# First attention of a two-layer block, from tokens on partitions to channels on partitions

## The chip, the cores and the metric

The kernel runs on one core of a Trainium2 chip. The core has five engines with a queue each: TensorE (PE; its weight loads are listed apart as PEld), VectorE (DVE), ScalarE (ACT), GpSimd (POOL) and SyncE (SP), which here only issues transfers. An engine works its queue off in order and waits on semaphores where an instruction needs another engine's result. Sixteen DMA engines move data between DRAM and the on-chip memory SBUF; TensorE writes to the banks of PSUM.

The metric is the device time of one execution in microseconds, as the median over runs. Before the change it is 2111.85 us (18 runs, 2101.27 to 2121.52).

## What is computed

Two layers with a layer norm after each sublayer, over 16 sequences of 512 tokens and 128 channels, in float32:

```python
x = L0_attn_x
x = _layernorm(x + _L0_attn_ref(x, ...), axis=-1)
x = _layernorm(x + _L0_ffn_ref(x, ...), axis=-1)
x = _layernorm(x + _L1_attn_ref(x, ...), axis=-1)
x = _layernorm(x + _L1_ffn_ref(x, ...), axis=-1)
```

The change is in the first attention. It has 16 heads of 64 value channels, 1024 in all, and is linear in time:

```python
cross = jnp.einsum('bnw,hw->bhn', x, k1) + p1
diag = jnp.einsum('bnw,hw->bhn', x, k2)
extra = jnp.einsum('bnw,hw->bhn', x, k3)
values = jnp.einsum('bnw,hwa->bhna', x, value_weight)
cexp = lambda z: jnp.exp(jnp.clip(z, -20.0, 20.0))[..., None]
cross, diag, extra = (cexp(cross), cexp(diag), cexp(extra))
p2e = cexp(p2)
num = jnp.cumsum(cross * values, axis=2) * p2e * extra + values * diag
den = jnp.cumsum(cross, axis=2) * p2e * extra + diag
out = num / den
return jnp.einsum('bhna,hwa->bnw', out, output_weight)
```

The running sum goes over the tokens of a sequence (axis 2). Every gate (`cross`, `diag`, `extra`, `p2e`, and so `1/den`) is one number for each head and token, the same for the head's 64 channels. The other sublayers are a mixture of eight experts with one expert a token, a softmax attention of 16 heads with a position bias, and a second mixture with a shared expert. They are not changed.

## The kernel before

The kernel does not run the sublayers one after the other. Every piece of work is an `op` with an engine, a planned cost and the tiles that it reads and writes, and all are issued in one order, which is written out as a long string, `ORDER` (L54 to L206): two characters for each op give its rank. Each engine gets its ops in that order. The string comes from a search outside the kernel; nothing of it is computed at build time. When an op is added or removed, the whole string is another one.

The sequences go in chunks (`CHUNKS`, L32: 2, 3, 4, 3, 3 and 1). `first` runs the first attention and first mixture of a chunk, `second` its softmax attention and what the shared expert needs, `mixture1` the routed part of the second mixture. The first layer of chunk c+1 is woven into the second attention of chunk c, so that both share the engines: only chunk 0's first layer has nothing beside it but the setup, and after the last chunk's first layer the second attention runs on without it.

Tiles come from pools with a fixed number of buffers (L285 to L311). The ones that matter here: `pair`, two banks of PSUM, 3 buffers; `wide`, 128x1024 float32 in SBUF, 12 buffers; `one`, one bank of PSUM, 2 buffers; `row`, 128x512 in SBUF, 11 buffers. They are shared by all sublayers.

The first attention of a sequence is `attention0`, then four tiles of 128 tokens by `tile0`. Tokens lie on the partitions. `attention0` makes the gates as 128 tokens x 4 tiles x 16 heads: scores (L952 to L957), exponentials in `ex`, prefix sums of `cross` by products with a triangle of ones (`ce`, L966 and L968), and from these `gg` = p2e·extra/den and `own` = diag/(cross·den) (L976 to L990). `tile0` then does for each tile of 128 tokens:

- `pv` (L1015, PE): values of all 1024 channels, two products 128x512
- `ev` (L1028, DVE): values times `cross`, the gate repeated over a head's 64 channels by a stride of 0
- `self_` (L1034, POOL): `ev` times `own`
- from the second tile on, the last row of the tile before (`carry`, L1057, ACT) is added into row 0 of `ev` by an accumulating transfer that POOL issues (L1041)
- `cum` (L1050, PE): running sum along the tokens, a product with the triangle `tri`
- `o` (L1062 and L1066, DVE): `cum` times `gg`, plus `self_`
- `po` (L1073, PE) and `ot` (L1076, ACT): eight transposes, so that channels lie on partitions, and a copy
- `y` (L1081, PE) and the residual add (L1089, DVE): eight products 128x128 with the output weights, added to `x`

So the tiles of one sequence form a chain: tile t+1 needs the carry of tile t.

The second attention, which shares the engines with it, works in rounds: 16 a sequence, four groups of heads times four tiles of keys. A round has its scores (`st`, L1422, PE), the bias added (`p`, L1441, DVE), the exponential (L1447, ACT) and the weighted sum (`av`, L1456, PE), beside a pass in low precision that finds the maxima (`s`, L1308 and L1317, PE; `low`, L1333, ACT, and L1349 to L1377, DVE). q and k of a group are moved into place by SP (L1272, L1285), and the maxima go the same way (`mx`, L1405): the scores of a group wait for that last transfer of 8 KB, which is planned 1.5 rounds ahead (`EARLY`, L41). GpSimd issues the indirect transfers of the mixtures (L796): expert weights, and rows of tokens there and back.

Of the kernel before, what the change touches and what calls it, by code (L numbers as in the profile page):

```python
# [19 lines left out]
P = 128  # L20
# [34 lines left out]
    "#$###)#9#-#0#.#&#%#(#A#D#'#,#B#G#J#=#7#H#I#K#*#?#L#M#O#F#P#Q#R#W#X#Y#6#C#T#U#Z#<#>#S#a#d#@#3#[#i"  # L55
    "#k#N#4#^#f#m#`#g#l#n#o#t#{#}#/#2#1$-#s#x$4$2$/$c#_#5#r&:#+#:#;%H'Y#u#8#v#w#V#]#b#~$#$$#c#p$'$&$+"
    "$)$*$0$3$:$A#e#z$,$.$7$9$8$<$B$E$K$]$1$6$;$?$D$H$L$M$N$[$a$e$C$G$I$J$T$U$W$Y$b$h$u$y%'%J%Q%R%W%["
    "%l#E#|$F$O$P$S$V$Z$Q$R$f$X$^$`$g$j$k$q%5$_$d$i$m$n$o$v$w$x${%*%@$l$p$r$s$|%,%)%+%-%2%E%M$z%$%(%."
    "%/%6%8%<%A%B%K%N%S%X%Y%^%`%b%c%d%e%f%m&8&Q&q'2&9&?&>&G&H&I&U&Y'.&E&o&R&Z&t&{&}&~'5'$'&'%'3'>'@'P"
    "'['e'#']'T'V'h'n't'u'v(/(2(4(=(@(d(r(s*>+T#y#h#j#q$%$($5$=$t%w$>%1&7%v'A'f(I(G%y'*&i%x$@$}%z'B(>"  # L60
    ")5'?-.(K%t(B(C(S(W(D(O(T(P(N(Y)>)&)d)=(U(x(q(V([)T)e)S)g)<)J)K({(~)$)Q)*)+)-(l(z(})E)1)6)9)C)G)I"
    ")X)m)3):)@)/)2)4)H)r)u*)*;*L)')F(e(k)?)f)c*P*Z*T*U*f*_*w*})O)V)^)Y)Z)j)v*|*`*c*{+'+-+9)W)])i)7)8"
    ")D)x*o*n*t++*u+/+A)N)P)U)(),)0*,*3*z+#+(+>*~+8+K*(***0*#*$*'*5*6*7*S*[+&+N+Q+Y)a)b)R)`+*+5+I+4+G"
    "+H+L+_+P+[+k*:*=*@)s)t)y*A+@+R+X+a+D+W+p*<*B*E)w)z)|*F+E+`+d+s+F+Z+}*C*D*I*4*8*9*J*K+6+g+l+x+;+C"
    ",*)p)~*&*+*/*1*p*q*r*x*y+J,0,4,<*.*-*G*%+h,/,&+n,,+b+f+o,1,8,9*M*Y*^*g*h*i+0+r+w+z,2+v+{,:*]*a*b"
    "*d*e*l+=+i+|,#,@+m+y,C*k*m*s+$+%+.+2+B,%,),5,E,',3,P+1+:+?+)+7+<+O+U+c+t,$,(,X,],`,W,A,F,S,Z,b,m"
    ",N,O,U,d,R,g,w,l,Q,T,[,n,p,~,^,_,i,v,a,j-+-1-5-=-E-[-_-t-u.).8.J.K.u.}.W.r.[.`.x/5/;1H,+,-,e,f,."
    ",7,=,>,D,B,;,M,?,r,H,K,V,L,J-8,s-9-W-/-4-<-2-3-;-O,u,{,}-'-)-0-K-?-A-C,|-#-*-Q-X-&-(-,,h,o,x-R-Y"
    "-Z.$.%.+,I,z,y,q-I---:-V.A.@.I.L.D.Y.c-L-P-`-6-@-B-m.M.S.U.a.O.X.p-d-f-h-J-M-]-p.Q.d.g.s.V.b.~-G"
    "-S-^-e-i-l-n-o.k.h.m.n.t.y/E-a-c-g-s-x-y-z.0.3.B.G.^/F/O/b-U-T-k-H/R.q/V/T/#/I/J/_/'/B/f.,.-.5-v"  # L70
    "-}-~/,/?/K/Q/^/G/H/p.>.E.H./.=.?.j/M/`/g/r/W/d/{.w.z.{.v.|/%/-/./o/h/k/s/v/}/~.e.f.i.6.7.9.l///0"
    "/@/D/j0#0005._.C-{.Z0$0%0+0,/y/w/x0;0)0K0O/$/&/)/*/+/1/<070*0/0J090I0U/(/2/6/[/a/e/i/z030?0Z0.0E"
    "0]/4/8/=/7/>/C/P/U0A0H0P0_0G0Q0b/L/N/]/X/c/q0'0(060=0F0L0q0u0z0W0M0S0T0X0`0k0N0R0V0a0^0h0l0[0i0r"
    "0t0m0o0|0d0n0y1%0v1'1(1)1,1.1415181@1A1C1N1Q1R1^1a1]1b1`1d1g2s3-:{$~%#%%%&%0%4%7%9%3%:%;%?%I%C%D"
    "%F%O%a%i%=%>%L%P%V%_%Z%]%o%{%|&.%T%U%g%h%j&$%n%u&&&'&)&+%p%q%s&%&*&/&2&3&6&=&S'8'F'Z(.(1(8(H%k%r"
    "%G%}%~&#&,&1&;&(&-&A&0&5&<&B&C&F&j&k&4&@&J&K&L&N&V&W&[&c&d&p&D&M&O&P&a&f&g&h&l&r'1'7&`&e&s&w&x&y"
    "&z'+'4':'G'H'L'i'}(#(g(m&X&T&]&^&_&b&u&v&m&n&|'''-'(')'6'9'M'N','/'='D'E'O'J'K'Q'S'a'k';'<'I'R'W"
    "'X'_'`'g'y'z($'U'^'p'q'w'x'|'~()(+(,(-(E(X(f(h(n(u(w(|)%).)[)k*?+~/:/A*R*j*v+,+M+V+e+j-7*Q+q+]+^"
    ",6,G,Y,k.*+3-%-D-F-q-w.;.</Y-b.P...:/3/9/S/Z/t/l/m/n/|0102080>0C0D0{0~1#1+0x1w1x424H1B2Q2m4^5R1j"
    "1y2.221k1l2F3#1m3$3=3;3W3[3]3_3c3d3g3m4%7)3X4*3z3{4?4B4@4L4M4X4e8:4{5D5k5l5s6u5y6/6w7h7q7s6`8(7v"  # L80
    "7y9a9s9i9j9t:2:F:[;s=I>/DhDiI@IA<;=9=T>5>??QBg/u10132b3'161=1:1<171D1G1c1r1s1F1v1L1|1J1u2'3J2~2C"
    "2G2K2L2P2W2p2=2@2B2D2E2J2d2M2V2Z2X2]2f3%322^2_2i2j2l2q3435363I3Q3R1[1P1O1T1~3b1q1}3k3e3j3t3n3v4&"
    "2,2/211o2#2$294)3p3u4+4.464:252:2;1f1h1i2<3l4345473o3x4C1z1{2(2024262R2S404;4A4I484F4T232>2?2H2I"
    "2N2O2T2U383G3P4Y4[4`2`2c2|2}4N4Q4G4R4V3w3y4>4Z4f4i3(3*3+2z3,313D4D4$4-4K4P4a4m2o2t2w373<3@3E4_4W"
    "4]4s4b4t5&303:3>3A3B3F3K3L4j4g4o4z4k4w5'2u2y3&3.3/393M3N3O4/4<4S5,54582Y2A2e2r4p4u4l4q4c5%5+514d"
    "4v592g2h2k2a2v2x334n5)5.524}5(5@3H3T3Y3S3U3a3f555*5-535:5;5A3h3i3q3V3Z3^3s3|4x505>5F4y5$5J3}3~4#"
    "4'4(4,444E4J4h4r4|5K5P5b5G5<5?5d5L5`5~5Q5E5N5V5S5u6$5}5x5{6'6#606;5T6%6.635e5t6R6Z6h6i7#7:7D7E7F"
    "7L7u7}7~9r9|878=8C8G8H8Y8]98575H616<5M5Z5X5U5Y5p5|6&6*6+5^6)5z5c5_6E7>6=7'6K6M6U6>6C6O6X65696:62"
    "67686p6^6c6g6L6N6]6j6l6?6D6G6A6F6J7-7.707`7a7r6_6,6(5a6P7(6B748-7{8#8I868;8L6z6|6~6n6r6t788%8/85"
    "8a8&8+8j6o6s6v6b6f6m6x8O8R8U8c8S8e8k6}71777$7,737S7T8f8X8`8p8g8u8v7=7A7C6{7+727G7_7m8081898{9496"  # L90
    "6k6q797%9m9.9l928V8m8o8|8W8d9+7B7M7O767?7@7d8l8t8y9$8x9)9@7]7f7g7I7N7R7k9#8}9'9,909L9d7n7w7z7p7|"
    "8*8.8?8w9?9A9^8~9D9g7U7W7Z7V7Y7[7l8A979O9W9y9p9v9w7J7t7K7<9n9q9o9_:&9z:$:,:':.:K8E8J8M7^7b7i8N:9"
# [183 lines left out]
def block_kernel(ctx: ExitStack, tc: tile.TileContext, d, out: bass.AP):  # L276
# [661 lines left out]
    def attention0(b, x, xt, span):  # L938
# [20 lines left out]
        def part(i):  # L959
            return ex()[:, :, i * H0 : (i + 1) * H0]  # L960
# [1044 lines left out]
```

## Time and profile before

| | us |
|---|---|
| median of 18 runs | 2111.85 |
| profiled execution, its own time | 2114.21 |
| its span, first to last instruction | 2112.4 |
| first instruction L1015 (`pv`) / last | 41.8 / 1547.0 |
| first instruction L1441 (softmax scores) / last | 320.5 / 2024.3 |
| mean granted clock of TensorE | 0.975 |

The page has six parts. Part 1 gives each engine's busy time, its share of the span and its instructions. Part 2 cuts the span in 40 equal slices and gives the busy share of each in tenths. Part 3 lists the transfer queues: q1 holds what SyncE issues, q0 what GpSimd issues. Part 4 follows the chain of work that ended last. Part 5 groups instructions by line, engine and tile: a group's line has the busy time and the mean duration of one in ns, then the idle time of the engine just before them and what ended it. Part 6 lists the transfers.

A float32 product appears twice in the counts, as two passes, so the 128 products `pv` are listed as x256. Busy time is a union: where instructions overlap, it is less than the number times the mean. A table of stages gives for each stretch the busy time of each engine with the number of instructions in brackets, then the granted clock, the share of the sixteen transfer engines, and GB/s.

### The profile page before, as it was taken

How to read it: one execution, taken by the hardware profiler on the slowest of the kernel's cores; microseconds unless marked ns; L12 is line 12 of the kernel's file. 1: busy time of each engine (PE TensorE's matmuls, PEld its weight loads, DVE VectorE, ACT ScalarE, POOL GpSimd, SP SyncE). 2: the span in 40 equal slices, each digit the busy share in tenths (PEclk: the TensorE clock that was granted, in tenths of full speed). 3: DMA queues.
4: the chain of work that ended last, by engine and by line, in shares of the span. 5: the costliest groups of instructions: out<-in, count | busy, mean ns of one | idle time of the engine just before them, and what ended most of it. 6: DMA issues, size and time to landing. Idle time of an engine off the chain costs nothing. (4 is left out here: it accounts for less than half of the span.)

```text
span 2112.4 us, 32135 instructions
## 1 busy us (share of the span) xinstructions
PE 1930.7 (91%) x11437; PEld 1039.4 (49%) x11437; DVE 1680.3 (80%) x2894; ACT 1496.7 (71%) x2066; POOL 799.0 (38%) x879
## 2 busy tenths in 40 slices
PE   4888998999999999899999999999999899999888
PEld 1566644444555454445454543456445444443465
DVE  8565578787979878798888697978868798989856
ACT  5222368886877678577779788767687799899653
POOL 5235551325222533632224344543332654131433
PEclk9899999999999999999999999999999999999899
DMA  4414533422331344334034432233154445443353
GB/s 122 139 38 114 155 114 117 153 76 95 116 119 50 107 140 121 107 117 120 23 106 132 143 111 91 88 101 113 42 177 129 142 134 160 142 121 107 92 172 101
DMA packets 188579, 240.09 MB, mean 114 GB/s; under 512 B 22148, under 2 KB 132612, under 8 KB 188420
## 3 DMA queue, kind: packets, MB, share of 16 engines
q1 hardware_dynamic: 162868, 149.36, 23.5%
q0 software_dynamic: 25552, 88.68, 13.9%
q8 instruction: 91, 1.49, 0.3%
q14 instruction: 68, 0.56, 0.1%
HBM read 164.50 MB, written 80.42 MB: 116 GB/s over the span
## 5 line engine op out<-in xcount | busy, mean ns | idle before, releaser
L1441 DVE TENSOR_TENSOR p<-st,bias 128x1024 f32<-128x1024 f32 x512 | 605.7, 1215 | 52.9 <-PE st L1422 44.0
L1333 ACT CAST low<-s 128x1024 bf16<-128x1024 f32 x512 | 499.5, 1020 | 127.0 <-PE s L1317 120.6
L1447 ACT ACTIVATE p<-p 128x1024 f32<-128x1024 f32 x512 | 521.9, 1060 | 76.6 <-DVE p L1441 70.1
L796 POOL DMA_INDIRECT ws<-tab,rows x201 | 204.7, 1018 | 399.2 <-DVE yq L1153 178.4
L1308 PE MATMUL s<-bias,ident 128*128 128x512 bf16 x1024 | 307.2, 394 | 27.4 <-ACT low L1333 15.0
L1456 PE MATMUL av<-p,vaug 128*32 128x512 f32 x2048 | 268.7, 605 | 2.4 <-ACT p L1447 1.5
L1422 PE MATMUL st<-qk_pad 64*128 64x512 f32 x1024 | 226.7, 477 | 33.2 <-DVE p L1441 16.5
L1034 POOL TENSOR_TENSOR self<-ev,own 128x1024 f32<-128x1024 f32 x64 | 125.1, 1957 | 300.9 <-DVE ev L1028 122.5
L1349 DVE TENSOR_TENSOR low<-low 128x1024 bf16<-128x1024 bf16 x256 | 183.3, 723 | 45.5 <-ACT low L1333 42.8
L1422 PEld LDWEIGHTS st<-qk_pad 64*128 64x128 f32 x1024 | 90.3, 185 | 212.2 <-DVE p L1441 84.7
L796 POOL DMA_INDIRECT yg<-results,place x124 | 124.9, 1008 | 120.5 <-issue 51.4
L1308 PEld LDWEIGHTS <-ident 128*128 128x128 bf16 x1024 | 86.0, 99 | 168.1 <-issue 139.7
L1317 PE MATMUL s<-qk_pad 32*128 32x512 bf16 x1024 | 148.2, 387 | 0.1
L1050 PE MATMUL cum<-ev,tri 128*128 128x512 f32 x256 | 127.5, 622 | 13.6 <-DMA ev<-carry 10.8
L1081 PEld LDWEIGHTS y<-ow,ot 128*128 128x128 f32 x1024 | 123.7, 196 | 20.2 <-issue 13.5
L1081 PE MATMUL y<-ow,ot 128*128 128x128 f32 x1024 | 131.3, 283 | 1.4 <-DVE ex L953 0.6
L1015 PE MATMUL pv<-vw,xt 128*128 128x512 f32 x256 | 128.5, 627 | 1.2 <-ACT low L1333 0.5
L1062 DVE TENSOR_TENSOR o<-cum,gg 128x1024 f32<-128x1024 f32 x64 | 78.2, 1221 | 64.2 <-ACT carry L1057 35.3
L626 POOL TENSOR_SCALAR rs<-mv 128x4 f32<-128x4 f32 x63 | 19.9, 315 | 258.9 <-DVE mv L620 254.8
L1028 DVE TENSOR_TENSOR ev<-pv,ex 128x1024 f32<-128x1024 f32 x64 | 77.8, 1218 | 47.6 <-PE pv L1015 47.1
L1076 ACT COPY ot<-po 128x1024 f32<-128x1024 f32 x64 | 64.9, 1014 | 70.5 <-PE po L1073 62.8
L1317 PEld LDWEIGHTS <-qk_pad 32*128 32x128 bf16 x1024 | 35.2, 91 | 147.3 <-issue 141.2
(226 smaller groups left out, 3143.3 us busy)
## 6 DMA issues: line engine op xcount, KB each, us to landing
qk_pad<-parts SPq DMA_DIRECT2D x256, 128.0 KB
parts<-lo SPq DMA_DIRECT2D x32, 512.0 KB
parts<-hi SPq DMA_DIRECT2D x32, 512.0 KB
xq<-tokens SPq DMA_DIRECT2D x42, 256.0 KB
results<-yq SPq DMA_DIRECT2D x42, 256.0 KB
bias<-rows SPq DMA_DIRECT2D x16, 448.0 KB
x<-in_x SPq DMA_DIRECT2D x16, 256.0 KB
xt<-in_xt SPq DMA_DIRECT2D x16, 256.0 KB
```

The costliest lines, as they stand in the source:

```text
L796: nc.gpsimd.indirect_dma_start(out, bass.IndirectOffsetOnAxis(to, 0) if to is not None else None, in_, bass.IndirectOffsetOnAxis(of, 0) if ...
L1015: nc.tensor.matmul(pv()[:, hf, :], xt()[:, col(t)], vw[:, hf * N : (hf + 1) * N], start=True, stop=True,)
L1050: nc.tensor.matmul(cum()[:, hf, :], tri, ev()[:, hf, :], start=True, stop=True)
L1081: nc.tensor.matmul(y()[:, :P], ot()[:, hf, col(c)], ow[:, 4 * hf + c, :], start=(hf == 0 and c == 0), stop=(hf == 1 and c == 3),)
L1308: nc.tensor.matmul(s()[:, i, :], ident16, bias16[:, 4 * g + 2 * jp + i, 2 * u + 1 : 2 * (u + N) : 2], start=True, stop=False,)
L1317: nc.tensor.matmul(s()[:, i, :], pad[r, 0, col(it)], pad[r, 1, :], start=False, stop=True,)
L1333: lambda s=s, jp=jp, low=low: nc.scalar.copy(low().bitcast(BF16).rearrange("p i (j n) -> p (i j) n", j=2)[:, 2 * jp : 2 * jp + 2, :], s(),),
L1349: nc.vector.tensor_tensor(to[:, :, h * (it // 2) : h * (it // 2) + h], v[:, :, :h], v[:, :, h:], ALU.max)
L1422: nc.tensor.matmul(s[jp]()[:, i, :], pad[r, 1, jp, col(jt)], pad[r, 0, jp, :], start=True, stop=True,)
L1441: lambda jp=jp, h=h, pj=pj: nc.vector.tensor_tensor(pj(), s[jp](), bias[:, h : h + 2, u : u + N], ALU.add),
L1447: ACT, 1.0, lambda pj=pj: nc.scalar.activation(pj(), pj(), AF.Exp),
L1456: nc.tensor.matmul(acc()[32 * j : 32 * j + 32, :], va[:, jt, h * VW : h * VW + 32], p[j // 2]()[:, j % 2, :], start=(jt == 0), stop=(jt == ...
```

## The change

Channels go on the partitions, from the value product on, and a unit of work is no longer a tile of 128 tokens with all heads but four heads with all 512 tokens: `heads0` in the place of `tile0`, again four units a sequence.

- With the running sum divided by `cross`, S[n] = (cross[n-1]/cross[n])·S[n-1] + v[n], and the output is gg·cross·S + diag·v/den. So three gates are needed for each head and token: the ratio of neighbouring `cross`, `own` and the factor of the sums.
- The gates are made as before with tokens on partitions, then turned by four transposes a sequence (`tp`), copied (`rows`), the ratios formed, and written to DRAM (`gates0`, two transfers).
- For each unit three transfers spread a gate's four heads over 128 partitions x 1024 (`ratio`, `own`, `sums`; each row goes to 64 partitions).
- VectorE scans along the tokens, `tensor_tensor_scan` over `ratio` and the values in PSUM, and multiplies `own` by the values; GpSimd multiplies `sums` by the scan and adds `own`.
- The result is already as the output product needs it. The triangle product, the carry with its transfer, the transposes back and their copy go. The residual is added for 512 tokens at a time.
- Value and output weights get the new order of channels: the value weights by four copies on ScalarE, the output weights by four transfers.
- `ORDER` is another string, found for durations that were disturbed at random. Other functions keep their text.

```diff
-            nc.vector.reciprocal(own(), part(0))
-            nc.vector.tensor_tensor(own(), own(), part(1), ALU.mult)
+            nc.vector.reciprocal(part(2), part(0))
...
+            nc.vector.tensor_tensor(part(1), part(1), den(), ALU.mult)
             nc.vector.tensor_tensor(gg(), gg(), den(), ALU.mult)
-            nc.vector.tensor_tensor(own(), own(), den(), ALU.mult)
+            nc.vector.tensor_tensor(part(3), gg(), part(0), ALU.mult)
...
+        def turn():
+            for t in range(NT):
+                nc.tensor.transpose(tp()[: 4 * H0, col(t)], ex()[:, t, :], ident)
+        op(PE, 0.44, turn, reads=[ex], writes=[tp])
+        op(
+            ACT, 0.5, lambda: nc.scalar.copy(rows()[: 4 * H0], tp()[: 4 * H0]), reads=[tp],
+            writes=[rows],
+        )
+        def ratios():
+            to = rows()[4 * H0 : 5 * H0]
+            nc.vector.memset(to[:, 0:1], 0.0)
+            nc.vector.tensor_tensor(
+                to[:, 1:], tp()[2 * H0 : 3 * H0, 1:], rows()[:H0, : N - 1], ALU.mult
+            )
...
+        for f, first, n, key in ((0, 4 * H0, H0, (rows, 1)), (1, H0, 3 * H0, rows)):
+            op(
+                SP, 0.48,
+                lambda f=f, first=first, n=n: nc.sync.dma_start(
+                    gates0[b % 2][f * H0 : f * H0 + n], rows()[first : first + n]
+                ),
...
+    def heads0(b, s, x, xt):
...
+        for f, to in ((0, ratio), (1, own), (3, sums)):
+            def spread0(f=f, to=to):
+                nc.sync.dma_start(
+                    flat(to),
+                    gates0[b % 2][f * H0 + 4 * s : f * H0 + 4 * s + 4]
+                    .rearrange("(q i) n -> q (i n)", i=2).unsqueeze(0)
+                    .to_broadcast([A0, 2, 2 * N]),
+                )
...
+            for i in range(2):
+                nc.tensor.matmul(
+                    pv()[:, i, :], vw[:, (2 * s + i) * P : (2 * s + i + 1) * P], xt(),
+                    start=True, stop=True,
+                )
...
+            DVE, 2.2,
+            lambda: nc.vector.tensor_tensor_scan(
+                flat(ratio), flat(ratio), flat(pv), 0.0, ALU.mult, ALU.add
+            ),
...
+            DVE, 1.15, lambda: nc.vector.tensor_tensor(own(), own(), pv(), ALU.mult),
...
+            POOL, 2.0, lambda: nc.gpsimd.tensor_tensor(sums(), sums(), ratio(), ALU.mult),
...
+            POOL, 2.0, lambda: nc.gpsimd.tensor_tensor(sums(), sums(), own(), ALU.add),
...
+            for t in range(NT):
+                for i in range(2):
+                    nc.tensor.matmul(
+                        y()[:, col(t)], sums()[:, i, col(t)], ow[:, 2 * s + i, :],
+                        start=(i == 0), stop=(i == 1),
+                    )
...
+            DVE, 0.6, lambda: nc.vector.tensor_tensor(x(), x(), y(), ALU.add),
```

## The prediction, made before the changed kernel had run

> **What bounds the kernel now.** I read the page's busy shares first, then its forty slices, then a table of stages, then the groups of instructions, and last the queue of SyncE.
>
> ```profile
> PE 1930.7 (91%) x11437; PEld 1039.4 (49%) x11437; DVE 1680.3 (80%) x2894; ACT 1496.7 (71%) x2066; POOL 799.0 (38%) x879
> PE   4888998999999999899999999999999899999888
> DVE  8565578787979878798888697978868798989856
> ```
>
> TensorE is busy 91% of the span, and near full in almost every slice but the first. The stages follow: up to the first softmax score of layer 1 (A, 0 to 320 us), while first-attention tiles still run (B, to 1550), the last of them (to 1640), the rest, and a stretch of pure second attention.
>
> ```profile
> core 0: us, PE busy (x) PEld busy (x) DVE busy (x) ACT busy (x) POOL busy (x), PEclk, DMA share, GB/s
> 0.00:320.00 320.00, 254.94 (x1245) 158.79 (x1245) 201.77 (x372) 127.43 (x179) 150.36 (x161) 0.93 0.40 113
> 320.00:1550.00 1230.00, 1160.11 (x6997) 608.18 (x6997) 1023.11 (x1708) 936.29 (x1282) 440.74 (x467) 0.99 0.35 106
> 1550.00:1640.00 90.00, 86.80 (x591) 50.85 (x591) 70.00 (x112) 71.40 (x109) 26.19 (x29) 1.00 0.45 130
> 1640.00:2112.00 472.00, 428.84 (x2610) 221.62 (x2608) 385.38 (x705) 361.62 (x497) 181.68 (x223) 0.97 0.43 131
> 1700.00:1950.00 250.00, 240.45 (x1512) 110.84 (x1509) 223.47 (x351) 230.72 (x307) 79.72 (x97) 1.00 0.44 131
> ```
>
> B is bound by TensorE: 1160 of 1230 us, 94.3%; VectorE has 83.2%, ScalarE 76.1%. The last row shows how full several engines can be together: 96.2%, 89.4% and 92.3%. The chain that ended last covers only the end of the span, where the change has nothing, so I do not build on it.
>
> **The change, part by part.** The groups that go, and the rows that price what comes:
>
> ```profile
> L1050 PE MATMUL cum<-ev,tri 128*128 128x512 f32 x256 | 127.5, 622 | 13.6 <-DMA ev<-carry 10.8
> L1066 DVE TENSOR_TENSOR o<-o,self 128x1024 f32<-128x1024 f32 x64 | 83.1, 1298 | 6.2 <-POOL self L1034 3.3
> L1062 DVE TENSOR_TENSOR o<-cum,gg 128x1024 f32<-128x1024 f32 x64 | 78.2, 1221 | 64.2 <-ACT carry L1057 35.3 <-PE cum L1050 27.1 <-PE av L1456 1.6
> L1073 PE MATMUL po<-ident,o 128*128 128x128 f32 x512 | 70.2, 282 | 17.6 <-DVE o L1066 14.6 <-ACT low L1333 1.4 <-DVE den L985 0.5
> L1057 ACT COPY carry<-cum 32x1024 f32<-32x1024 f32 x48 | 48.2, 1004 | 74.4 <-DVE o L1062 37.8 <-PE cum L1050 22.9 <-issue 13.0
> L744 DVE TENSOR_TENSOR_SCAN upto<-fresh,cnt 128x96 f32<-128x96 f32 x6 | 2.1, 357 | 0.2
> L754 DVE TENSOR_TENSOR_SCAN end<-ones,size 128x8 f32<-128x8 f32 x11 | 1.9, 175 | 0.4
> L1524 DVE TENSOR_TENSOR x<-x,y 128x512 f32<-128x512 f32 x16 | 10.9, 684 | 12.7 <-PE y L1520 12.7
> q1 hardware_dynamic: 162868, 149.36, 23.5%
> SPq L1405 <- ACT mx L1400: 279.2, 46, 25.3
> ```
>
> *TensorE.* The prefix sums (127.5 us) and the transposes back (70.2) go. The value products stay two 128x512 products a unit (128.5 us in all), only with the operands swapped; the output products stay eight 128x128 (131.3). New are four transposes a batch: 64 at 70.2/512 = 0.137 us, 8.8 us. Net -189 us. By stage, the same two groups restricted to A hold 52.0 + 27.5 us, to B 73.5 + 40.5, afterwards 4.1. B's demand becomes 1160.1 - 114.1 + 38 x 0.137 = 1051 us.
>
> *VectorE.* A unit loses L1028 (1218 ns), L1062 (1221), L1066 (1298) and L1089 (279): 4.02 us. It gains a scan over 1024, a product from PSUM, priced as L1028 (1.22), and an add of 128x512 priced as L1524 (0.68). The scan rows are 357 ns at 96 elements and 175 at 8, so 2.07 ns an element and 0.175 + 1016 x 0.00207 = 2.28 us at 1024: against 1.22 for a plain operation. Sum 4.18 us, +0.17. A batch also gains the 16x511 product (0.68), one 128x64 product (0.22) and a memset (at most 0.16, as an eight-element operation) and loses L978 (0.22): +0.84, or +0.21 a unit. So +0.38 us a unit, +24 in all, and B demands 1023.1 + 38 x 0.38 = 1038 us.
>
> *ScalarE* loses the carry copies (48.2) and L1076 (64.9), gains 16 copies of 128x512 at L1467's 586 ns: -104 us. In B, 936 - 28.1 - 38.5 + 5.6 = 875.
>
> *GpSimd* loses 48 accumulating transfers (L1041, 43.2 us), keeps one 128x1024 product a unit (L1034, 1957 ns) and gains one add of that size: +125 - 43 = +82 us. In B 440.7 + 75.9 - 26.5 = 490, 43% of a shorter stage: hidden by its own idle time. But each unit's result now needs both GpSimd operations, 3.9 us, behind whatever that queue waits for (the weight fetch L796 waited up to 27.5 us for L1153). With that cover gone one unit is late by that much, and the next output product and residual add with it; the TensorE work queued behind them waits too.
>
> [...]
>
> *Transfers.* 192 spreads of 512 KB (0.524 MB), three a unit, are 100.7 MB. Queue q1 moved 149.36 MB in 23.5% of 2112 us, 496 us of all engines, so 1.74 us each, 334 us together; the mean load goes from 38% to (798 + 334)/2000 = 57%. The 32 writes of gates are small. SyncE issues 224 more, at 0.4 to 0.6 us (medians of L1285 and L1248), some 112 us of a queue that mostly waits. Every one of them stands in the same in-order queue as the moves of q and k and as the shift (L1405), so it can hold these up, or be held up by them. Its cover is that they are issued ahead of use; what the loss of it costs is the second rival.
>
> *Bookkeeping at the start.* Four copies reorder the value weights on ScalarE (at most 4 x 0.59 us) and the output weights come in four transfers instead of one; the first value product was at 41.8 us, and ScalarE had 28 of the first 50 us. Nothing.
>
> **The sum.** A: the first two batches' attention ran from the gates at 57.8 us to the last residual add at 140.5, along the serial carry chain. New: 57.8 + 0.6 transposes + 0.6 copy + 0.7 product + 3.5 for the write (as the first load, issued at 1.3 and landed at 4.8) = 63.2; 24 spreads of 1.74 are 42, to 105; the last unit's 1.7 + 2.3 + 3.9 + 2.0 + 0.7 = 10.6, to 116. Other loads take 0.46 of the engines from 50 to 100 us and 0.20 to 150, up to 33 us more. So -24 to +8; I take -12, and no gain from the 180 us of routing and experts after it, whose chain has latencies that stay.
>
> B: TensorE 1051 and VectorE 1038 now have the same load. At the old share of 94.3% B takes 1115 us (-115), at the 96.2% seen elsewhere 1093 (-137), at 87% 1208 (-22). I take 92%, 1142 us, -88: below its own share because a second engine is equally full, above VectorE's best of 89.4% because that row shows three engines above 89% at once. After B: -2.
>
> 2112.4 - 12 - 88 - 2 = 2010 of span. The profiled execution took 2114.2 for a span of 2112.4, and the median of eighteen is 2111.9; so a median of 2009, rounded to 2008. The bounds of these terms give 1947 to 2094; the forecast's own range is 1960 to 2060.
>
> **The rivals.**
>
> *VectorE takes over and the gain is small.* Scans of 2.28 us block its queue twice as long as any operation there now, and scores (the weight loads of L1422 waited 84.7 us for L1441) wait behind them. If VectorE reaches only 87% in B: 1038/0.87 = 1193, -37, and A gives nothing: about 2075 (2060 to 2106). For it: its highest share in any stage above is 89.4%, in B 83.2%. Against: many of its waits in B are for the cum and carry that go (L1062's 64.2 us).
>
> *Slower: the spreads delay the shift.* One batch brings 12 x 1.74 = 21 us of transfers. The second attention starts at 320 and its last score sum is at 2024: 1704/256 = 6.7 us a round, and the shift (L1405) is planned 1.5 rounds ahead, 10 us. A whole batch issued in front of a shift makes it 11 us late, and the scores behind it and all of TensorE with them. Once for each of 14 batches: 154 us, 2010 + 154 = 2164. It makes the kernel slower from 102/14 = 7.3 us a batch on. For it: SyncE sat 279 us at the head of its queue for L1405's data, with everything behind it. Against: today TensorE waits 2.4 us in all for the moves of q and k, and the queue stays below 40% busy; in the new SyncE order the spreads mostly come one to three at a time between other transfers.
>
> *The full gain.* TensorE at 96.2% in B and A's -24: 2112 - 137 - 24 - 2 = 1949 of span, 1947. For it: a unit takes one of the three PSUM pairs once instead of three times, and the chain of carries through a transfer is gone.
>
> That the change does not do what it says I exclude: the built order has 64 scans, 192 spreads and no prefix product over channels.
>
> **How the numbers follow.** Forecast 0.46, small gain 0.16, full gain 0.11, slower by the spreads 0.24, no difference 0.03. So faster by over 0.2% 0.73, within 0.2% (4 us, about what this kernel's runs can tell) 0.03, slower 0.24. The range leaves 0.08 below 1950 and about 0.12 above 2130, half of the slower case.
>
> **What would show it.** Right: 1742 us of TensorE, 1704 of VectorE, 1393 of ScalarE, 881 of GpSimd; scans of 2.2 to 2.4 us; the first score sum near 308 us, and 565 us from the last value product to the end, as now. Wrong: scans well over 2.4 us (VectorE then bounds B); spreads that land later than 5 us after issue, with scans or L1422 waiting for transfers (the slower rival); or TensorE below 87% in B with no single wait that grew, which would mean that the order itself fits the chip worse.

## The result, and the profile after

The changed kernel takes 2165.28 us (median of 10 runs, 2153.93 to 2167.9), the kernel before 2112.98 beside it: 1.0239 times, interval [1.0222, 1.0255]. Forecast were 2008 us. The profiled execution took 2167.61 us for a span of 2165.9. From run 9 on the kernel before itself took 2150 to 2155 us in place of 2112 to 2115, so those runs are held by their ratio to a run of it beside them.

Busy times and slices of the changed kernel's page (busy share of 40 slices in tenths; PEclk is the granted clock):

```profile
PE 1866.2 (86%) x10733; PEld 980.0 (45%) x10733; DVE 1773.7 (82%) x2862; ACT 1396.5 (64%) x1974; POOL 936.4 (43%) x895
PE   5566778999798899789899998888999989999887
PEclk9677988999899999889999999899999899999999
DMA  4768874645463464345453643475464345343253
```

TensorE has 64 us less to do than before (1930.7), not 189. VectorE rose from 1680 to 1774, GpSimd from 799 to 936. TensorE, near full after the first slices before, now has slices of 7 and 8 tenths all through, and its granted clock falls with them, in the mean from 0.975 to 0.925.

The changed kernel by stages, cut as in the prediction at the first softmax score and behind the last value product:

```profile
core 0: us, PE busy (x) PEld busy (x) DVE busy (x) ACT busy (x) POOL busy (x), PEclk, DMA share, GB/s
0.00:338.00 338.00, 216.07 (x993) 138.30 (x993) 223.85 (x360) 89.67 (x147) 199.24 (x164) 0.81 0.70 225
338.00:1602.00 1264.00, 1136.93 (x6631) 574.71 (x6630) 1092.22 (x1694) 884.05 (x1234) 529.40 (x484) 0.94 0.50 154
1602.00:2166.00 564.00, 513.22 (x3112) 267.02 (x3110) 457.62 (x808) 422.73 (x595) 207.75 (x248) 0.96 0.42 129
```

A grew from 320.5 to 338.2 us (forecast 308), B from 1226.5 to 1264.2 (forecast 1142), C stayed (565 and 563). The loss against the kernel before is +18, +38 and -2; the loss against the forecast is +30, +122 and +2. So B is the question, then A.

Groups of the changed kernel (count | busy us, mean ns | idle before), the maxima being L1355:

```profile
L1079 POOL TENSOR_TENSOR sums<-sums,ratio 128x1024 f32<-128x1024 f32 x64 | 153.2, 2394 | 288.4 <-DVE ratio L1069 152.4
L1355 DVE TENSOR_TENSOR low<-low 128x1024 bf16<-128x1024 bf16 x256 | 211.7, 834 | 43.4 <-ACT low L1339 40.0
L1090 PE MATMUL y<-ow,sums 128*128 128x128 f32 x1024 | 150.3, 308 | 56.1 <-POOL sums L1083 51.4
L1069 DVE TENSOR_TENSOR_SCAN ratio<-ratio,pv 128x1024 f32<-128x1024 f32 x64 | 145.9, 2280 | 24.5 <-PE pv L1057 12.1
L1083 POOL TENSOR_TENSOR sums<-sums,own 128x1024 f32<-128x1024 f32 x64 | 154.7, 2419 | 20.0 <-issue 10.6
L1057 PE MATMUL pv<-xt,vw 128*128 128x512 f32 x256 | 136.3, 659 | 18.1 <-ACT vw L1824 14.7
```

and of the kernel before, GpSimd's product and the same maxima:

```profile
L1034 POOL TENSOR_TENSOR self<-ev,own 128x1024 f32<-128x1024 f32 x64 | 125.1, 1957 | 300.9 <-DVE ev L1028 122.5
L1349 DVE TENSOR_TENSOR low<-low 128x1024 bf16<-128x1024 bf16 x256 | 183.3, 723 | 45.5 <-ACT low L1333 42.8
```

The scan costs what was priced (2280 ns). Two things do not fit: GpSimd's operations take 2.39 and 2.42 us, not 1.96, and the bf16 maxima of the second attention, which the change does not touch, went from 723 to 834 ns (L1349 before). All maxima together (512) went from 351.8 to 399.8 us.

How a VectorE operation gets longer shows in the timeline, at the first routing, where the mixture picks each token's expert (start us, duration us). VectorE of the changed kernel:

```profile
142.61 0.22 DVE L698 TENSOR_REDUCE m<-lg 128x8 f32<-128x64 f32 x1
142.87 2.30 DVE L699 TENSOR_TENSOR oh<-lg,m 128x64 f32<-128x64 f32 x1
145.20 2.38 DVE L700 TENSOR_TENSOR oh<-oh,rev 128x64 f32<-128x64 f32 x1
147.62 0.22 DVE L701 TENSOR_REDUCE f<-oh 128x8 f32<-128x64 f32 x1
```

and GpSimd of the same kernel at the same time:

```profile
142.75 2.34 POOL L1079 TENSOR_TENSOR sums<-sums,ratio 128x1024 f32<-128x1024 f32 x1
145.16 2.34 POOL L1083 TENSOR_TENSOR sums<-sums,own 128x1024 f32<-128x1024 f32 x1
```

Two VectorE operations of 64 elements, 0.22 us each in run 1 below, end 80 ns after the GpSimd operation that began before them. They wait for nothing that the page lists as a wait: the time is booked as busy VectorE. The two reductions beside them last 0.22 us, as in run 1.

### The profile page after: what moved, and what is told of

It reads as the page before. It is cut to its first block, busy times and chain, and to the rows that moved or that the text cites. A ratio compares the mean times of both kernels' runs of the same rounds, so it can differ in the third digit from the quotient of the medians.

```text
span 2165.9 us, 31014 instructions
## 1 busy us (share of the span) xinstructions
PE 1866.2 (86%) x10733; PEld 980.0 (45%) x10733; DVE 1773.7 (82%) x2862; ACT 1396.5 (64%) x1974; POOL 936.4 (43%) x895
## 5 line engine op out<-in xcount | busy, mean ns | idle before, releaser
L1447 DVE TENSOR_TENSOR p<-st,bias 128x1024 f32<-128x1024 f32 x512 | 605.6, 1215 | 58.3 <-PE st L1428 49.6
L1428 PE MATMUL st<-qk_pad 64*128 64x512 f32 x1024 | 237.2, 491 | 47.8 <-DVE p L1447 26.5
L1079 POOL TENSOR_TENSOR sums<-sums,ratio 128x1024 f32<-128x1024 f32 x64 | 153.2, 2394 | 288.4 <-DVE ratio L1069 152.4
L1355 DVE TENSOR_TENSOR low<-low 128x1024 bf16<-128x1024 bf16 x256 | 211.7, 834 | 43.4 <-ACT low L1339 40.0
L1090 PE MATMUL y<-ow,sums 128*128 128x128 f32 x1024 | 150.3, 308 | 56.1 <-POOL sums L1083 51.4
L1090 PEld LDWEIGHTS y<-ow,sums 128*128 128x128 f32 x1024 | 140.7, 220 | 76.0 <-POOL sums L1083 59.8
L1323 PE MATMUL s<-qk_pad 32*128 32x512 bf16 x1024 | 165.6, 404 | 1.2 <-DMA qk_pad<-rounds 1.2
L1069 DVE TENSOR_TENSOR_SCAN ratio<-ratio,pv 128x1024 f32<-128x1024 f32 x64 | 145.9, 2280 | 24.5 <-PE pv L1057 12.1
L1083 POOL TENSOR_TENSOR sums<-sums,own 128x1024 f32<-128x1024 f32 x64 | 154.7, 2419 | 20.0 <-issue 10.6
L1057 PE MATMUL pv<-xt,vw 128*128 128x512 f32 x256 | 136.3, 659 | 18.1 <-ACT vw L1824 14.7
L636 ACT ACTIVATE x<-x,rs 128x128 f32<-128x128 f32 x192 | 79.0, 486 | 54.9 <-POOL rs L629 50.6
L929 PE MATMUL py<-ws,h 128*128 128x128 f32 x804 | 105.0, 285 | 5.4 <-DVE h L1553 2.8
```

The source lines that it names most:

```text
L929: nc.tensor.matmul(py()[:, col(s)], h()[:, c, col(s)], ws[s]()[:, off + c * W : off + (c + 1) * W], start=(c == 0), stop=(c == 1),)
L1083: POOL, 2.0, lambda: nc.gpsimd.tensor_tensor(sums(), sums(), own(), ALU.add),
L1090: nc.tensor.matmul(y()[:, col(t)], sums()[:, i, col(t)], ow[:, 2 * s + i, :], start=(i == 0), stop=(i == 1),)
L1323: nc.tensor.matmul(s()[:, i, :], pad[r, 0, col(it)], pad[r, 1, :], start=False, stop=True,)
L1355: nc.vector.tensor_tensor(to[:, :, h * (it // 2) : h * (it // 2) + h], v[:, :, :h], v[:, :, h:], ALU.max)
L1428: nc.tensor.matmul(s[jp]()[:, i, :], pad[r, 1, jp, col(jt)], pad[r, 0, jp, :], start=True, stop=True,)
```

## The experiments

Theories at the start: V, GpSimd's doubled work stretches VectorE, which becomes the limit of B; T, the 100 MB of spreads crowd or come late; G, TensorE waits in A for GpSimd's pair and its clock falls; O, the order does not fit this chip's durations.

**1. Without both GpSimd operations.**

```diff
-            POOL, 2.0, lambda: nc.gpsimd.tensor_tensor(sums(), sums(), ratio(), ALU.mult),
+            POOL, 2.0, lambda: None,
...
-            POOL, 2.0, lambda: nc.gpsimd.tensor_tensor(sums(), sums(), own(), ALU.add),
+            POOL, 2.0, lambda: None,
```

> The changed kernel without both GpSimd operations of a unit (128 of some 2.4 us, 308 us): the output product takes the gates of `sums` as they were spread, so the products with the running sum and with the own value are left out of the result; spreads, scans and order stay. Theory V (VectorE became the limit, because GpSimd's big operations stretch its maxima with two SBUF inputs): VectorE's busy time falls by some 48 us to about 1725, the maxima L1355 from a mean of 834 to under 720 ns, B (338 to 1605 us) shortens by 45 to 60 us; about 2165 - 50 - 15 (A) = 2100. Theory T (transfers late): at most the GpSimd waits go, 2155 to 2165. Theory G (TensorE waits for the GpSimd pair in stage A, its clock falls there): A shortens by 30 to 60 us and B by less than 10: 2100 to 2135, told from V by the stages. Theory O (the order does not fit the durations of this chip): GpSimd's 2.4 us in place of the planned 2.0 is gone, VectorE keeps its busy time, and B shortens by under 15.

Measured: 2070.83 us, 0.9807 [0.9781, 0.9834]. Stage B of this run:

```profile
322.00:1512.00 1190.00, 1095.24 (x6560) 563.89 (x6631) 1026.66 (x1694) 883.24 (x1234) 341.11 (x407) 0.97 0.53 163
```

A went from 338 to 322, B from 1264 to 1190, VectorE in all from 1774 to 1684 and in B from 1092 to 1027, the maxima L1355 to 706 ns and all 512 maxima from 400 to 338 us. The same two operations at the routing take 0.22 us here. More than V had expected (2100): B lost 74 us for 66 us of VectorE, A 16 us. C, which the edit does not touch, is 10 us shorter too (553; 558 in the changed kernel of run 5).

**2. Without the add alone.**

```diff
-            POOL, 2.0, lambda: nc.gpsimd.tensor_tensor(sums(), sums(), own(), ALU.add),
+            POOL, 2.0, lambda: None,
```

> The changed kernel without GpSimd's add of the own values alone (64 of 2.42 us, 155 us); the own values are left out of the result, the product that makes them stays on VectorE. Theory V: half of what the run without both gives, VectorE -25 us, about 2130. Theory G: half of stage A's wait (111 us of TensorE for GpSimd's result over the kernel), about 2145, all of it in A. Theories T and O: 2155 to 2165.

Measured: 2104.32 us, 0.9958 [0.9937, 0.9979]; A 324, B 1221, all maxima 360 us. V, with a larger size: B -43 for 38 us of VectorE. The second GpSimd operation of a unit costs more than the first, which alone has 31 us of B (1221 to 1190).

**3. A plain product for the scan.**

```diff
-            lambda: nc.vector.tensor_tensor_scan(
-                flat(ratio), flat(ratio), flat(pv), 0.0, ALU.mult, ALU.add
-            ),
+            lambda: nc.vector.tensor_tensor(ratio(), ratio(), pv(), ALU.mult),
```

> The changed kernel with a plain product in place of the scan (same operands, 1024 elements): the running sum over the tokens is left out. An operation of 1.21 instead of 2.28 us, 64 times: VectorE's busy time falls by 68 us, 40 of them in B. Theory V: B shortens by 40 or more, about 2115. Theories T and G: A by the 1.07 us of a unit's chain at most, 2150 to 2165. Theory O: 2150 to 2165, since the order stays. The maxima keep their mean of 834 ns, as GpSimd still does as much.

Measured: 2132.18 us, 1.0092 [1.0066, 1.0118]. A stays at 338, B falls to 1235: 29 us for 44 us of VectorE. VectorE's own work is paid, at some 0.65, but not in full; V had expected 40 us or more.

**4. One spread a unit in place of three.**

```diff
         for f, to in ((0, ratio), (1, own), (3, sums)):
...
             def spread0(f=f, to=to):
+                if f:
+                    return to()
...
-            DVE, 1.15, lambda: nc.vector.tensor_tensor(own(), own(), pv(), ALU.mult),
+            DVE, 1.15, lambda: nc.vector.tensor_tensor(flat(own), ow.rearrange('p k w -> p (k w)'), flat(pv), ALU.mult),
...
-            POOL, 2.0, lambda: nc.gpsimd.tensor_tensor(sums(), sums(), ratio(), ALU.mult),
+            POOL, 2.0, lambda: nc.gpsimd.tensor_tensor(sums(), ratio(), ratio(), ALU.mult),
```

> The changed kernel with one spread a unit in place of three (64 of 192, 67 MB fewer): the own product takes the output weights as its SBUF operand and GpSimd squares the running sum, so the gates of the own value and of the sum are left out; every engine does as many operations of the same size. Theory T (transfers crowd or come late): q1 falls from 37 to some 27 % of 16 engines, stage A, where the transfers hold 0.70 of the engines, shortens by 20 to 40 us, B by 10 or more: 2105 to 2135. Theories V and O: 2155 to 2168, VectorE and the clock as they were. Theory G: the GpSimd product no longer waits for its gates (49 us in all), 2145 to 2160.

Measured: 2113.46 us, 1.0004 [0.9992, 1.0017]: A 317, B 1234.5. T's total, but its edit had a second effect, which GpSimd's groups in this run show:

```profile
L1085 POOL TENSOR_TENSOR sums<-sums,own 128x1024 f32<-128x1024 f32 x64 | 153.8, 2405 | 19.7 <-DVE own L1077 10.1 <-DVE gates L1013 6.0
L1081 POOL TENSOR_TENSOR sums<-ratio 128x1024 f32<-128x1024 f32 x64 | 123.8, 1935 | 287.0 <-DVE ratio L1071 165.4 <-PE av L1464 34.5 <-ACT mx L1408 22.8
```

An operation that reads one tile twice takes 1935 ns, one with two tiles 2405. So this run also took 29 us from GpSimd and 14 from the maxima, and what it says of transfers in B is open. Run 6 is the clean one.

**5. The changed kernel beside the next three.**

> The changed kernel itself, unchanged, beside the runs below on one chip. All theories: 1.024 times the kernel before, 2160 to 2167. It sets the stages that the variants are held against: the stage after the last value product, which no variant touches, was 563 us in the first profile of the changed kernel and 553 to 558 in the four variants; if it is 553 to 558 here too, 8 us of each variant's difference belong to the chip and not to the variant.

Measured: 2158.83 us, 1.0193 [1.0132, 1.0254]; A 342, B 1263, C 558. The last stage of the variants of runs 1 to 7 is the same within some 5 us, so the stages above may be compared.

**6. Without GpSimd's pair and with one spread**, that of `sums`. GpSimd's lines as in run 1, and:

```diff
+                if f != 3:
+                    return to()
...
-                flat(ratio), flat(ratio), flat(pv), 0.0, ALU.mult, ALU.add
+                flat(ratio), ow.rearrange('p k w -> p (k w)'), flat(pv), 0.0, ALU.mult, ALU.add
...
-            DVE, 1.15, lambda: nc.vector.tensor_tensor(own(), own(), pv(), ALU.mult),
+            DVE, 1.15, lambda: nc.vector.tensor_tensor(flat(own), ow.rearrange('p k w -> p (k w)'), flat(pv), ALU.mult),
```

> The changed kernel without GpSimd's two operations and with one spread a unit (that of the sum's gates, which the output product takes as they are; scan and own product take the output weights as their SBUF operand). Left out: the gates of scan and own value, and GpSimd's products. VectorE, ScalarE and TensorE do as many operations as the changed kernel. If the costs of GpSimd's operations (92 us of time without them) and of the transfers (50 us) are separate, 2165 - 92 - 50 + 15 (the part of stage A that both gave) = 2040, 2030 to 2050. If both act through one thing (a late result of the unit), 2060 to 2075. My prediction's own sum without its two mis-sized costs, 2008 + 0 to 20, would be 2008 to 2030.

Measured: 2033.26 us, 0.962 [0.9576, 0.9664]. Stages A and B of this run:

```profile
0.00:291.00 291.00, 208.20 (x993) 133.76 (x993) 203.49 (x360) 89.46 (x147) 80.65 (x113) 0.86 0.59 167
291.00:1476.00 1185.00, 1098.03 (x6633) 560.26 (x6632) 1027.72 (x1694) 883.22 (x1234) 343.17 (x408) 0.98 0.43 131
```

The two costs are separate, as expected. Against run 1, two spreads less a unit bring 31 us in A (322 to 291) and 5 in B (1190 to 1185). So without GpSimd's pair the transfers cost nearly nothing outside A.

**7. Every value product twice.**

```diff
-            for i in range(2):
+            for i in (0, 1, 0, 1):
                 nc.tensor.matmul(
                     pv()[:, i, :], vw[:, (2 * s + i) * P : (2 * s + i + 1) * P], xt(),
```

> The changed kernel with every value product made twice, to the same PSUM tile: 2 more products of 128x512 a unit, 128 of 0.63 us or 81 us of TensorE in all, 48 of it in B. Theory V (VectorE limits B, TensorE idles beside it): up to +25 us, 2165 to 2190, TensorE's idle time takes it up and its granted clock in B rises from 0.94. If TensorE limits B after all: +50 to +80 us, 2215 to 2245, with the clock as it was.

Measured: 2219.18 us, 1.0503 [1.0444, 1.0561], 60 us more than run 5. TensorE's busy time rose by 101 us, in B by 62 (1130 to 1192), B by 46 (1263 to 1308) and A by 11, and the clock in B stayed at 0.95. V's prediction of +25 us falls: VectorE is not the limit that leaves TensorE idle. Work added on TensorE is paid, as work taken from VectorE is gained.

**8. The kernel before with its GpSimd product made twice.**

```diff
-            lambda: nc.gpsimd.tensor_tensor(split(self_), split(ev), heads(own(), t), ALU.mult),
+            lambda: [nc.gpsimd.tensor_tensor(split(self_), split(ev), heads(own(), t), ALU.mult) for _ in range(2)],
```

> The kernel before, with GpSimd's product (L1034, 128x1024, 1957 ns) made twice, with the same result: GpSimd has as many big operations as the changed kernel, 64 more, and nothing else changes. Theory V's cost by itself: the maxima go from 352 to 370 to 400 us of VectorE; the unit's chain is 2 us longer, 64 times. If that decides, 2130 to 2170. If the kernel before is bound by TensorE and its order carries it, 2112 to 2125, and the loss in the changed kernel needs VectorE's share beside it. [...]

Measured: 2168.93 us, 1.0267 [1.022, 1.0313]. The repeated operation and the largest group of maxima in it:

```profile
L1034 POOL TENSOR_TENSOR self<-ev,own 128x1024 f32<-128x1024 f32 x128 | 258.6, 2022 | 269.3 <-DVE ev L1028 87.2 <-PE av L1456 50.2 <-DVE own L990 26.0
L1349 DVE TENSOR_TENSOR low<-low 128x1024 bf16<-128x1024 bf16 x256 | 195.1, 770 | 43.0 <-ACT low L1333 40.1
```

Sixty-four more operations of 2 us on an engine with 38% cost the old kernel 54 us, as much as the whole change. It has no scan, no spread and its own order, so a loss of this size does not need the new order (O). The maxima went from 352 to 373 us, `o + self` (L1066) from 83 to 92. B is 30 us longer (1227 to 1257) for 24 us more of VectorE, in line with V; A is 21 us longer (320 to 342). The later result of each unit, by 2 us, is a rival that this run does not exclude, in A above all, which holds the chains of the first eight units.

**9 and 10. GpSimd's results written where nobody reads them.** The output product takes `sums` as spread and waits for no GpSimd result; GpSimd works as much, with two tiles in SBUF.

```diff
-            POOL, 2.0, lambda: nc.gpsimd.tensor_tensor(sums(), sums(), ratio(), ALU.mult),
+            POOL, 2.0, lambda: nc.gpsimd.tensor_tensor(ratio(), sums(), ratio(), ALU.mult),
...
-            POOL, 2.0, lambda: nc.gpsimd.tensor_tensor(sums(), sums(), own(), ALU.add),
+            POOL, 2.0, lambda: nc.gpsimd.tensor_tensor(own(), sums(), own(), ALU.add),
```

> The changed kernel with GpSimd's two operations written to tiles that nobody reads (ratio takes sums x ratio, own takes sums + own): the same 128 operations with two operands in SBUF run at the same places of GpSimd's queue, but the output product takes the gates of `sums` as spread and waits for no GpSimd result; the products with running sum and own value are so left out of the result. Beside it stand the changed kernel (2159 to 2165) and the one without these operations (2071). If the loss is the stretching of VectorE's operations that have two SBUF inputs, VectorE's busy time stays near 1770 and the time at 2140 to 2160, B at 1245 to 1265. If the loss is that the unit's result comes later (two operations of 2.4 us before the output product), VectorE is stretched all the same, but the time falls to 2075 to 2095, B to 1190 to 1205. Stage A, where TensorE waits for the pair, 322 to 330 by either.

Measured: 1.0363 [1.0288, 1.0437], without the changed kernel beside it; so once more with it:

> The changed kernel with GpSimd's two operations writing to tiles that nobody reads, as before (running sum and own value left out of the result), now with the changed kernel on the same chip. Stretching as the cause: 0.98 to 1.01 times the changed kernel, B as long as there within 20 us. The late result as the cause: 0.96 or less, B shorter by 60 us or more.

> The changed kernel itself, beside the three runs below on one chip: 1.02 to 1.026 times the kernel before by every theory.

Measured: the unread results 1.0305 [1.025, 1.036], the changed kernel 1.0332 [1.03, 1.0363]. Stage B of the run with unread results,

```profile
329.00:1632.00 1303.00, 1130.52 (x6560) 573.74 (x6631) 1085.41 (x1693) 885.68 (x1234) 526.24 (x484) 0.94 0.48 149
```

and of the changed kernel beside it:

```profile
342.00:1641.00 1299.00, 1132.06 (x6556) 578.38 (x6629) 1083.85 (x1693) 885.00 (x1234) 526.64 (x482) 0.94 0.48 149
```

The rows agree within 1%. In B nobody's wait for GpSimd's result matters; it is enough that the operations run. They still keep their tiles from coming free here; runs 13 and 14, where GpSimd takes longer and the kernel less, speak against that as the cause. In A, where TensorE does wait for it, 12 us are gained (342 to 329). G is right there and only there.

**11. The add on VectorE.**

```diff
-            POOL, 2.0, lambda: nc.gpsimd.tensor_tensor(sums(), sums(), own(), ALU.add),
+            DVE, 1.3, lambda: nc.vector.tensor_tensor(sums(), sums(), own(), ALU.add),
```

> The changed kernel with the add of the own values on VectorE in place of GpSimd (same result): GpSimd loses 155 us, VectorE gains 64 adds of 128x1024 with two SBUF inputs, 1.30 us each by L1066 of the kernel before, 83 us, and gets back some 39 us of stretching. The run without the add took 57 us less than the changed kernel; the run with a plain product for the scan showed 0.6 us of time for each us of VectorE in B. So 2162 - 57 + 0.6 x 83 = 2155. If stretching is paid in full and VectorE's own work is not, 2110 to 2130. If VectorE is the limit and its work is paid in full, 2160 to 2190.

Measured: 2247.0 us, 1.0488 [1.043, 1.0545], above every expectation (2190 at most, 1.036 times the kernel before). The maxima fell to 357 us, but the add took 81. The loss against the changed kernel of run 10 is all in A, 368 us against 342, and why A grew is not shown. B is as long with the add on either engine (1301 and 1300), with VectorE at 1093 and 1085 us there.

**12. The kernel before with its GpSimd product on VectorE.**

```diff
-            lambda: nc.gpsimd.tensor_tensor(split(self_), split(ev), heads(own(), t), ALU.mult),
+            lambda: nc.vector.tensor_tensor(split(self_), split(ev), heads(own(), t), ALU.mult),
```

> The kernel before with its one big GpSimd operation, L1034 (64 of 1957 ns), on VectorE (same result): VectorE gains 64 of some 1.22 us, 78 us, less the stretching that goes (the maxima from 352 to 338 us, L1066 by some 9). The same operation made twice on GpSimd cost 54 us. If each GpSimd operation costs 0.84 us of time whatever stands beside it, 2114 - 54 + 0.6 x 55 = 2093; if the kernel before has room for one such operation a unit and not for two, 2114 + 0.6 x 55 = 2147.

Measured: 2181.72 us, 1.0187 [1.0128, 1.0246]. The maxima fell to 335 us and L1066 to 78, but VectorE's total rose by 49, to 1730, and the time by 1.9%, some 40 us (31 by the two medians). That is near the second expectation (2147 of 2114 is 1.016): the kernel before has room for one such operation a unit, and pays for the second. Moving the work to VectorE made both kernels slower.

**13 to 15. GpSimd's operations in pieces** (for n pieces, of 1024/n elements; here n is 4).

```diff
-            POOL, 2.0, lambda: nc.gpsimd.tensor_tensor(sums(), sums(), ratio(), ALU.mult),
+            POOL, 2.0, lambda: [nc.gpsimd.tensor_tensor(flat(sums)[:, k : k + 256], flat(sums)[:, k : k + 256], flat(ratio)[:, k : k + 256], ALU.mult) for k in range(0, 2 * N, 256)],
```

and the add in the same way.

> The changed kernel with each of GpSimd's two operations cut into two of 128x512 (same result). If an operation of VectorE with two SBUF inputs waits until the GpSimd operation under way has ended, its longest wait falls from some 2.4 to 1.3 us, the maxima's excess over 338 us from 62 to 30 to 45 us, and the time by 15 to 40 us, 2120 to 2150 where the changed kernel has 2162, if GpSimd's total grows by less than 40 us. [...]

> The same in four pieces of 128x256 (same result). If whole operations are waited for: longest waits of 0.7 to 0.9 us, the maxima's excess 15 to 30 us, 2090 to 2135, with GpSimd's total 50 to 80 us longer. [...]

> The changed kernel with each of GpSimd's two operations in eight pieces of 128x128 (same result). By the runs in two and four pieces (GpSimd's pair 4.8, 5.2 and 6.0 us a unit, the maxima's excess over 338 us 50, 42 and 29 us, 1.033, 1.024 and 1.016 times the kernel before) a piece more costs GpSimd 0.2 us, so the pair takes some 7.7 us, and the excess falls to 15 to 25 us. If the stretch decides and the longer pair is hidden: 1.005 to 1.015. If the later result takes over: 1.016 to 1.03.

Measured, with the changed kernel in the first row:

```
pieces  GpSimd's 128 results, us   maxima, us   longest L702, ns   longest L1382, ns   time / before
1       306.8                      387.7        2359               3253                1.0332 [1.0300, 1.0363]
2       332.7                      380.0         949               5592                1.0244 [1.0217, 1.0271]
4       385.1                      367.4         394               6147                1.0158 [1.0105, 1.0210]
8       460.6                      368.8         539               7261                1.0345 [1.0306, 1.0384]
```

VectorE in the run with four pieces, at the routing shown above:

```profile
145.12 0.72 DVE L699 TENSOR_TENSOR oh<-lg,m 128x64 f32<-128x64 f32 x1
145.88 0.65 DVE L700 TENSOR_TENSOR oh<-oh,rev 128x64 f32<-128x64 f32 x1
```

The same operations now last 0.72 and 0.65 us, less than one piece (773 and 792 ns in the mean) instead of one operation of 2.34: the time they were held became as short as a piece. GpSimd works 78 us longer in four pieces, VectorE 31 us less (1765 to 1734), and the kernel is still 1.7% faster than the changed one beside it (1.0158/1.0332; 1.4% by the medians). With eight pieces the excess falls no further and A grows to 361 us: both my expectations, 1.005 to 1.015 and 1.016 to 1.03, were wrong. The longest wait did not fall as expected either. With eight pieces a result one operation of L1382 lasted 7261 ns, about as long as all sixteen pieces of a unit's two results, 7.20 us in the mean (460.6/64) (min/median/max ns of L1382):

```profile
L1382 DVE TENSOR_TENSOR low<-low x128: 424/612/7261, 341.6 to 2115.5; 128x1024 bf16<-128x1024 bf16 x64, 128x512 bf16<-128x512 bf16 x64
```

With four pieces it was 6147 ns, where a unit's pair takes 6.02 us, with two 5592, where it takes 5.20. With whole operations of 2.40 us the longest was 3253, and without the pair (run 1) 693.

**16. The kernel before with its product in four pieces.**

```diff
-            lambda: nc.gpsimd.tensor_tensor(split(self_), split(ev), heads(own(), t), ALU.mult),
+            lambda: [nc.gpsimd.tensor_tensor(split(self_)[:, k : k + H0 // 4], split(ev)[:, k : k + H0 // 4], heads(own(), t)[:, k : k + H0 // 4], ALU.mult) for k in range(0, H0, H0 // 4)],
```

> The kernel before with its product L1034 cut into four pieces of 4 heads each (same result). Its maxima take 352 us, against 335 to 338 where GpSimd does no big operation, and L1066 83 against 78: an excess of some 20 us, of which four pieces should take half. If the stretch is paid one to one as in the changed kernel: 0.993 to 0.997. If the longer product (4 x 0.2 us more) matters more, 1.000 to 1.006.

Measured: 0.9974 [0.9958, 0.999]; the maxima went from 352 to 346 us while GpSimd's product rose from 125 to 163. The same stretch, smaller, is in the kernel before. This version beats the kernel before by 0.26%, at the edge of the expected 0.993 to 0.997.

## Why the prediction was wrong

*The step that failed* is GpSimd's: "In B 440.7 + 75.9 - 26.5 = 490, 43% of a shorter stage: hidden by its own idle time". VectorE's 1038 us in B and 1704 in all held nothing for GpSimd's second operation a unit. Shown: GpSimd's pair costs 74 us of B (run 1), nobody's wait for its result is in that (runs 9 and 10), and a second operation a unit costs the kernel before 54 us too (run 8), though the first costs it little (runs 12 and 16). VectorE has 54 us more in B than the sum's 1038 and 70 more in all than its 1704. Without the pair it has 66 and 90 less: 62 of the 90 in the maxima, 28 in other operations. The kernel before had a sign of it: its L1349 had a median of 684 ns and a mean of 723. Why the maxima lose so much more here than in run 8, where as many more operations cost them 21 us, was not tried by itself.

Which operations get longer the traces show. L699 and L700, of 0.22 us and with both inputs in SBUF, took 2.30 and 2.38 beside operations of 2.34 and ended 80 ns after them. The maxima L1355, again with two inputs in SBUF, had a mean of 834 ns with GpSimd's pair and 706 without it (run 1). The scan, the own product and L1447, whose second operand is in PSUM, stayed within 1% of 2280, 1205 and 1215 ns in every run, the reduction of the maxima (L1383) at 686. The 7.26 us of run 15 is many times the length of a piece there (484 and 489 ns in the mean). Why it took so long stays open.

*GpSimd's price* was 1957 ns an operation, from L1034. Measured 2394 and 2419, 58 us more for the 128, and GpSimd's total is 936 in place of 881. L1034's second operand is one value repeated over a head's channels. Run 4's 1935 ns for one tile read twice points to the second tile as what costs.

*VectorE* was put at 1704 us, is 1774, and without GpSimd's pair 1684, which also lacks the 22 us or so of stretch in the kernel before (run 12: maxima 352 to 335, L1066 83 to 78): the prices of scan, products and adds were right. *ScalarE* (1393, is 1396.5) and *C* (565, is 563) were right. A spread takes (805.7 - 496.4) us of q1 for 102.8 MB, 1.58 us for 512 KB against 1.74.

*TensorE's demand in B* was put at 1051 us. It is 1137, and 1098 with GpSimd's pair and two spreads gone. The share of 92% that I took for two equally full engines was right for that case: 1098 of 1185 is 92.7%. So of the 122 us that B missed, 74 are GpSimd's, 5 the spreads' and 43 TensorE's larger demand.

The 74 go with 40 us of TensorE's own busy time (1137 to 1098), at a granted clock that rises from 0.94 to 0.98; what of them is the clock's was not tried by itself. Of the other 47 us (1098 against 1051), part is in the second attention's products, which the change does not touch: over the whole kernel L1308, L1317, L1422 and L1456 are busy 951 us before (626 in B) and 983 in run 6, for as many products. The medians of value and output products in B are the same before and in the changed kernel (592 and 275 ns); their means are 606 and 280 ns before and 634 and 288 in the changed kernel, at clocks of 0.99 and 0.94. The means of the whole kernel (627 and 283 before, 653 and 295 in run 6, 659 and 308 in the changed kernel) come more from A, in the changed kernel 698 and 343 ns, at 0.81. Why these products are busy longer stays open.

*A* was put at -12 us and came at +18. The attention of the first two batches is done sooner, as forecast: the first routing operation L699 starts at 142.9 us, before at 148.7, 6 us sooner and not 12. Then "no gain from the 180 us of routing and experts after it, whose chain has latencies that stay" failed: from L699 to the first score 195 us instead of 172. Run 6 gives both parts back, L699 at 124.5 and 167 us behind it. Transfers filled 0.70 of the engines in A where 0.40 had been, and GpSimd's pair held TensorE there; its waits in A's second part (140 to 340 us) in the changed kernel, first the weight loads, then the matmuls:

```profile
PEld y L1090 <- POOL sums L1083: 26.1, 7, 10.8
PE y L1090 <- POOL sums L1083: 23.3, 6, 9.7
```

*The rivals.* "VectorE takes over" had its share, 87%, right (1092 of 1264 is 86.4%), but not its reason: scans are no longer than priced, and run 7 shows that VectorE alone is no limit. "The spreads delay the shift" does not appear: TensorE's waits for `qk_pad` transfers add up to under 6 us. The slower side had its chance for the wrong mechanism; that its 2164 us is the time measured is luck. What was measured, VectorE's own operations made longer by GpSimd's, had no case of its own.

*What kind of limit B has.* Each engine's busy time is paid in part: 0.65 of VectorE's (run 3), 46 us for 62 of TensorE's (run 7), some 1.1 of the time by which GpSimd's pair makes VectorE's longer (74 us for 66, run 1). With an order fixed for all engines and 87% to 92% on two of them, there was no engine whose time was free. That a new order, searched with the longer durations measured here, could win the gain back is possible and was not tried; so O's share of the 43 us is open.

## What to carry to other kernels

An engine's idle share does not make work on it free: GpSimd was busy 38% of the kernel before, and 64 more of its operations cost 54 us there (run 8). Ask what else gets longer while it runs. Before work goes to GpSimd, list VectorE's operations with two inputs in SBUF, and count, as an estimate from these runs, at least one whole GpSimd operation for each that can meet it: 0.22 us became 2.30 beside one of 2.34. The profile books this as busy VectorE, so look at the longest durations (L1382: 693 ns without the pair, 3026 with it), not at waits. If work must stay there, pieces of some 0.8 us did better here (1.0158 times the kernel before) than one of 2.4 (1.0332), and better than eight of 0.45 (1.0345).

## What the runs showed of the hardware that was not expected

- A GpSimd operation of two different tiles takes 2394 to 2419 ns for 128x1024 in the changed kernel, with the same tile twice 1935 (run 4), with one operand repeated 1957 (kernel before); cut in two, four and eight, 2.60, 3.01 and 3.60 us (runs 13 to 15).
- A VectorE operation with one tensor input in SBUF got longer too: in the changed kernel L749, of 8 elements, took 2164 ns once (median 172), beside a GpSimd operation that ended some 30 ns before it.
- In runs 13 to 15 one VectorE operation (L1382) lasted longer than any single piece of GpSimd's and about as long as a unit's pair: 5592, 6147 and 7261 ns, where the pair takes 5.20, 6.02 and 7.20 us in pieces of 1.3, 0.8 and 0.45 us.
